# Three edits to a planned order on one Trainium2 core: the last group's choice behind a block's gated product, the first rows a step later, x loads behind block rows

## Chip, cores and metric

The kernel runs on one core of one Trainium2 chip (trn2). The metric is the device time of one execution in microseconds, the median of several runs; lower is better. Engines are named as the profile names them: PE (TensorE matmuls) and PEld (its weight loads), DVE (VectorE), ACT (ScalarE), POOL (GpSimd), SP (SyncE, which here issues most of the DMAs).

## Reference

Two feed-forward half-steps with a causal attention between them, for x of shape 2 x 2048 x 256 in float32. Cut to what matters:

```python
def half_step(x):                    # x already layer-normed by the caller
    xln = ln(x, ln1_w, ln1_b)
    att_out = sigmoid(xln @ Wr) * (xln @ Wv) @ Wo
    state = xln @ Ws
    x = x + att_out
    h = ln(x, ln2_w, ln2_b)
    conf = sigmoid(h @ [conf_rwkv; conf_trans])           # three experts
    bids = conf * capital_shares * sigmoid(h @ w_diff) + h @ W_aff
    winner = argmax(bids)
    scale = conf[winner] / (conf[winner] + 1e-6)
    out_rwkv[e] = square(relu(h @ K_rwkv[e])) @ V_rwkv[e]  # e = 0, 1; 256 -> 1024 -> 256
    out_trans = (h @ W1 * sigmoid(state @ W2)) @ W3
    return x + all_out[winner] * scale
x = x + 0.5 * half_step(layernorm(x))
x = x + attention(layernorm(x))      # one head of 128, softmax over the causal past
x = x + 0.5 * half_step(layernorm(x))
```

Only the winner's output of a token counts, so the kernel computes each token's winner alone.

## The kernel before

All arithmetic is float32. The 4096 tokens are two segments of 2048 (one for each batch entry), and a segment is four groups of 512 tokens (four tiles of 128 rows). A half-step has two parts, which overlap.

The front (`front`, class `Group`) takes the eight groups, 0 to 3 of the first segment and 4 to 7 of the second, in turn: moments and norms (`start`, `norm1`, `norm2`), transposes (`columns`, L348), the products for sigmoid gate and value (`r` and `v`, L362 on PE, L427 on ACT, L433 on DVE: the gate product `gate_t`), `mix` (L443), and `route` (L469). Then `logits` (L496 to L509) and `choose` (L517 to L531: bids, winners, and running counts `upto`; its last winner instruction, L526, is kept as `lately["chosen"]`). `rank` (L537, L538) and `slot` turn counts into a place for each token, and `move` (L568) scatters the group's rows into `by_slot` in DRAM, sorted by expert. After the last group of a segment `finish` writes `steer`, the list of which block starts at which slot; SP reads its entries into registers (L932, L964).

The experts part (`experts`, class `Block`) works on blocks of 256 rows of one expert. Kinds are "gt" (the gated expert), "rw" (an rwkv expert) and "half" (128 rows). `load_rows` (L933) reads a block's rows from `by_slot` into one of three `rows_in` buffers; `load_weights` (L944, L946) reads an rwkv expert's `w_k` and `w_e`. `ready` prepares the rows (L976 on DVE, L977 on ACT), `columns` transposes them (L847 on PE, copied out by L354 on ACT), `first` does the first product (for a gt block two sets of matmuls at L863, the sigmoid L990 on ACT, and the gated product L995 on DVE; for an rwkv block L863, relu L1004, L1005), and `second` the second (L878) with `res` (L903) and the scatter to the result (L911 on POOL). The first segment's blocks are two gt and four rw, and the second's follow.

Each part is a Python generator, and the code around it interleaves them: while the front does the second segment's groups (4 to 7), the experts part begins on the first segment's blocks. The order on the engines comes from the order in which the generators record, rearranged by the framework's scheduler, so the number of bare `yield` steps decides what stands beside what. `PACE` is 3 (front steps for one experts step) and `PAUSE` is 6. `tc.issue_after(ins)` (in `behind`) puts an instruction behind another of the same engine, in order only, with no semaphore. Engines run their queues in order.

In `pipelined`, which runs the blocks, block n + 1's weights and block n + 2's rows are asked for when block n starts. Its head loads the rows of blocks 0 and 1, waits some steps, and calls `ready` and `columns` for block 0, bound behind the choice that was recorded last. Block 1's `ready` is also bound so; from block 2 on it is not.

PSUM has two pools: `p_mm` with six buffers for products and `p_tp` with two, which transposes (`ps_t`, `ps_bt`, `ps_route`), routing sums (`ps_rc`), ranks and counts share.

Near the end of the first half-step `ahead` fetches the four x groups of the first segment (`fetch`, L152, from `x_mid` where the blocks' results went) for the attention, and normalizes them (L281 and on) between the late blocks.

Of the kernel before, what the change touches and what calls it, by code (L numbers as in the profile page):

```python
# [78 lines left out]
def kernel(ctx: ExitStack, tc: tile.TileContext, a: dict, out: bass.AP):  # L79
# [13 lines left out]
    def token_tiles(t, g):  # L93
        return t[g * TG : (g + 1) * TG, :].rearrange("(t p) d -> p t d", p=P)
# [48 lines left out]
        eng.dma_start(t, ap.rearrange("(k p) n -> p k n", p=P))  # L143
        return t

    def fetch(work, seg, n, src, bufs, after=(), beside=None):

        rows = work.tile([P, TB, RW], F32, name="rows", bufs=bufs)
        seg["rows"].append(rows)
        seg["x"].append(rows[:, :, XR : XR + C])  # L150
        seg["in_rows"].append(rows)
        ins = nc.sync.dma_start(seg["x"][n], src).ins  # L152
        if beside is not None:
            tc.declare_no_dep(ins, group=beside, reason="what may still come there has it fetched again")
            tc.add_to_no_dep_group(beside, ins)
        wait_for(ins, after)
# [217 lines left out]
    class Group:  # L374
# [133 lines left out]
            else:  # L508
                nc.scalar.activation(self.conf, self.by_kind[:, 0 : E + 1, :], AF.Sigmoid)  # L509

        def choose(self):
            upto = self.seg["upto"]
            if self.n == 0 and self.seg["prior"] is not None:
                nc.vector.tensor_copy(upto[:, :, 0], self.seg["prior"]["upto"][:, :, ST])
            conf = self.conf[:, 0:E, :]
            bids = sort_pool.tile([P, E, TB], F32, name="bids")
            nc.vector.tensor_mul(bids, conf, shares)  # L517
            nc.vector.tensor_mul(bids, bids, self.conf[:, E : E + 1, :].to_broadcast([P, E, TB]))
            nc.vector.tensor_add(bids, bids, self.by_kind[:, E + 1 :, :])

            most = sort_pool.tile([P, 2, TB], F32, name="most")
            nc.vector.tensor_max(most, bids[:, 0:2, :], bids[:, 1:3, :])
            wins = self.wins = sort_pool.tile([P, E, TB], F32, name="wins")
            nc.vector.tensor_tensor(wins[:, 0, :], bids[:, 0, :], most[:, 1, :], ALU.is_ge)
            nc.vector.tensor_tensor(wins[:, 2, :], bids[:, 2, :], most[:, 0, :], ALU.is_gt)
            lately["chosen"] = nc.vector.scalar_tensor_tensor(  # L526
                wins[:, 1, :], wins[:, 0, :], 1.0, wins[:, 2, :], ALU.is_lt, ALU.subtract
            ).ins
            for t in range(TB):
                at = self.n * TB + t  # L530
                nc.vector.tensor_add(upto[:, :, at + 1], upto[:, :, at], wins[:, :, t])  # L531
# [216 lines left out]
    def front(work, segs, by_exp=-1, on_move=lambda: None, fill=()):  # L748


        todo = [
            Group(work, seg, n, (b * GB + n <= by_exp, b * GB + n < by_exp)) for b, seg in enumerate(segs) for n in range(GB)
        ]

        def at(i):
            return todo[i] if 0 <= i < len(todo) else None

        def move(group):
            group.move()
            on_move()  # L760

        todo[0].start()
        run(todo[0].norm1(TB // 2))
        yield
        todo[1].start()
        todo[0].columns()
        yield
        for m in range(KC):
            todo[0].r(m)
            yield  # L770
            todo[0].v(m)
            yield
        run(todo[1].norm1(0))
        for i, this in enumerate(todo):
            late, following, further = at(i - 1), at(i + 1), at(i + 2)
            if late and late.n == GB - 1:
                late = None
            this.route(0)
            if late:
                late.rank()  # L780
                yield
            this.mix()
            yield
            this.route(1)
            if following:
                following.columns()
                yield
            this.deviation()
            yield
            if following:  # L790
                following.r(0)
                yield

            if further:
                further.start()
                yield
            if late:
                late.slot()
                with tc.issue_after((further or this).guess):
                    move(late)  # L800
                yield
            this.norm2(late.made if late else None)
            this.logits()
            yield
            if following:
                following.v(0)
                yield
            this.choose()
            yield
            if following:  # L810
                following.r(1)
                yield
                following.v(1)
                yield
            if this.n == GB - 1:

                yield from fill
                if not following:
                    for _ in range(PAUSE):
                        yield  # L820
                this.rank()
                this.slot()
                yield
                move(this)
                yield from finish(this.seg)
            if further:
                yield from further.norm1(0, following.made)
                yield

    def experts(work, segs, dest, redo=None):  # L830
# [98 lines left out]
        def load_rows(b, at, n, c):  # L929

            rows = work.tile([P, NI, RW], F32, name="rows_in", bufs=3)[:, 0:n, :]
            slot = nc.sync.value_load(segs[b]["steer"][0:1, at : at + 1], min_val=0, max_val=SLOTS - BLK)  # L932
            ins = nc.sync.dma_start(rows[:, :, c:], slot_rows(slot, n, c)).ins  # L933
            if b == 0:
                moves = segs[1]["moves"]
                tc.declare_no_dep(ins, group=moves, reason="rows of the other segment's tokens")
                tc.add_to_no_dep_group(moves, ins)
            for seg in segs[: b + 1]:
                wait_for(ins, seg["moved"])
            return rows  # L940
# [8 lines left out]
        class Block:  # L949
# [36 lines left out]
            def first(self, following=None, early=False):  # L986

                if self.kind == "gt":
                    sig = work.tile([P, 2, BLK], F32, name="gt_sig", bufs=1)
                    nc.scalar.activation(sig, several(w_s2, 0, self.cols_y), AF.Sigmoid)  # L990
                    yield
                    if following:
                        following.ready(lately["chosen"] if early else None)
                    self.mid = work.tile([P, KC, BLK], F32, name="gated", bufs=2)
                    self.made = nc.vector.tensor_mul(self.mid, several(later["w_1"], 0, self.cols), sig).ins  # L995
                    yield
                    return
                n = self.cols.shape[2]
                self.mid = work.tile([P, HC, BLK], F32, name="hid", bufs=2)[:, :, 0:n]
                step = 2 * BLK // n  # L1000
                for j in range(0, HC, step):
                    ps = several(self.w[0], j, self.cols)
                    relu = work.tile([P, 2 * BLK], F32, name="relu", bufs=2).rearrange("p (j n) -> p j n", n=n)
                    nc.scalar.activation(relu, ps, AF.Relu)  # L1004
                    self.made = nc.vector.tensor_mul(self.mid[:, j : j + step, :], ps, relu).ins  # L1005
                    yield
                    if following and j == HC // 2 - step:
                        following.ready(self.made)
# [7 lines left out]
        def pipelined(todo):  # L1016

            todo[0].load_rows()
            todo[0].load_weights()
            yield  # L1020
            todo[1].load_rows()

            yield
            yield

            todo[0].ready(lately["chosen"])
            todo[0].columns()
            yield
            for i, block in enumerate(todo):
                if i + 1 < len(todo):  # L1030
                    todo[i + 1].load_weights()
                if i + 2 < len(todo):
                    todo[i + 2].load_rows()
                yield from block.first(todo[i + 1] if i + 1 < len(todo) else None, i == 0)
                if i + 1 < len(todo):
                    todo[i + 1].columns()
                    yield
                yield from block.second()
# [212 lines left out]
    with pool("experts0", "right") as expert_pool:  # L1251
# [63 lines left out]

        def ahead():
            for n in range(GB):
                fetch(front_pool, t0, n, token_tiles(x_mid, n), GB, s0["results"], s1["moves_out"])
                yield
            yield from normed()  # L1320

# [70 lines left out]
```

## Time and profile before

| | us |
|---|---|
| Median of 3 runs | 881.61 |
| The runs | 881.1, 881.61, 886.78 |
| The profiled execution, its own time | 888.6 |
| Its span, first to last instruction | 886.4 |
| PE busy, DVE busy, ACT busy, POOL busy in the span | 845.2, 467.0, 319.5, 184.8 |
| Mean granted PE clock | 0.987 |

Times in the profile are those of one profiled execution, in us from the start of its span. In a timeline line the first number is the start, the second the duration, then engine, source line, operation, the tile written and read, shapes, and how many instructions of the kind are merged; in brackets stands the idle time of that engine just before, and what ended it. A few stages to find one's way: the front of the first half-step runs alone until about 98, the experts part overlaps groups 4 to 7 until about 149, blocks alone run until 334, attention until about 625, and the second half-step repeats the pattern (groups 4 to 7 with blocks from about 640 to 692, blocks alone until 878).

### The profile page before, as it was taken

To read this page: it belongs to the slowest core of one execution; us is meant where nothing else is said; L and a number is where in the kernel's file an instruction comes from. 1 tells how busy PE (TensorE), PEld (TensorE's weight loads), DVE (VectorE), ACT (ScalarE), POOL (GpSimd) and SP (SyncE) were. 2 spreads that over 40 slices of the span, in tenths; PEclk is the share of its full clock that TensorE was granted. 3 is DMA by queue.
4 is the path that set the end of the run, shared out by engine and by line. 5 is a ranking of instruction groups with operands and counts; after the bars stand their busy time and mean duration, and the time that the engine had idled before them with its cause. 6 is when DMAs were issued, how large, how long until landed. Compare 5 with 4: busy or idle time off the path is not lost. (4 is left out here: it accounts for less than half of the span.)

```text
span 886.4 us, 12466 instructions
## 1 busy us (share of the span) xinstructions
PE 845.2 (95%) x4136; PEld 616.9 (70%) x4136; DVE 467.0 (53%) x1857; ACT 319.5 (36%) x694; POOL 184.8 (21%) x232
## 2 busy tenths in 40 slices
PE   6999999999999998999899999999999999999996
PEld 4556567888878895655565556556556788888885
DVE  3588867233235445577434676665866532233322
ACT  3333542333244332454333343433352233243321
POOL 3145244111131211001000102022223410221101
PEclk9999999999999998999999999999999999999998
DMA  9424637656188543000000001021374763539652
GB/s 296 168 96 180 250 128 269 235 174 230 49 317 288 168 141 102 1 0 1 0 1 1 1 0 72 24 96 72 122 261 176 254 224 133 181 103 329 202 166 71
DMA packets 66370, 123.71 MB, mean 140 GB/s; under 512 B 4718, under 2 KB 44526, under 8 KB 66288
## 3 DMA queue, kind: packets, MB, share of 16 engines
q1 hardware_dynamic: 55856, 87.46, 29.5%
q0 software_dynamic: 8384, 33.70, 9.6%
q10 hardware_dynamic: 2048, 1.58, 0.6%
q8 instruction: 37, 0.61, 0.3%
q14 instruction: 45, 0.37, 0.1%
HBM read 82.47 MB, written 38.68 MB: 137 GB/s over the span
## 5 line engine op out<-in xcount | busy, mean ns | idle before, releaser
L863 PE MATMUL ps_b<-cols,w_k 128*128 128x256 f32 (+1 forms) x768 | 157.4, 363 | 0.0
L878 PE MATMUL acc<-w_e,hid 128*128 128x256 f32 x704 | 156.5, 379 | 0.0
L863 PEld LDWEIGHTS ps_b<-cols,w_k 128*128 128x128 f32 x768 | 137.4, 191 | 17.2
L878 PEld LDWEIGHTS acc<-w_e,hid 128*128 128x128 f32 x704 | 131.5, 190 | 17.3 <-DVE hid L1005 0.6
L291 POOL TENSOR_TENSOR r<-ve,mhalf 128x4 f32<-128x4 f32 (+1 forms) x40 | 50.9, 1272 | 380.9 <-DVE ve L332 291.0
L1004 ACT ACTIVATE relu<-ps_b 128x512 f32<-128x512 f32 x88 | 52.0, 591 | 171.4 <-PE ps_b L863 171.3
L1005 DVE TENSOR_TENSOR hid<-ps_b,relu 128x512 f32<-128x512 f32 x88 | 60.7, 690 | 80.3 <-ACT relu L1004 78.0
L903 DVE SCALAR_TENSOR_TENSOR res<-acc,rows_in 128x256 f32<-128x256 f32 x68 | 30.1, 479 | 119.8 <-PE acc L878 119.8
L1195 PE MATMUL ps_o<-p_tr,v 128*128 128x512 f32 (+3 forms) x160 | 73.4, 544 | 6.1 <-DVE p_tr L1189 2.9
L568 POOL DMA_INDIRECT by_slot<-rows,slots x64 | 62.5, 977 | 32.5 <-issue 27.0
L362 PE MATMUL ps_p<-y_t,w_r 128*128 128x512 f32 x128 | 64.8, 625 | 1.0 <-ACT y_t L417 0.9
L911 POOL DMA_INDIRECT out_dram<-res,where x34 | 33.5, 986 | 152.4 <-DVE res L903 139.3
L1141 PE MATMUL ps_s<-k_t,q_t 128*128 128x512 f32 (+3 forms) x160 | 64.2, 529 | 0.0
L443 PE MATMUL acc<-w_o,gate_t 128*128 128x256 f32 x256 | 61.2, 390 | 2.0 <-DVE gate_t L433 2.0
L362 PE MATMUL ps_p<-y_t,w_v 128*128 128x512 f32 x128 | 62.3, 607 | 0.0
L911 POOL DMA_INDIRECT x_mid<-res,where x34 | 33.7, 993 | 128.5 <-DVE res L903 123.4
L1158 ACT ACTIVATE prob<-ps_s,shift 128x512 f32<-128x512 f32 (+3 forms) x72 | 43.6, 615 | 43.5 <-DVE shift L1154 43.5
L1150 DVE TENSOR_REDUCE top<-ps_s 128x1 f32<-128x512 f32 (+2 forms) x80 | 48.4, 606 | 15.4 <-PE ps_s L1141 14.5
L443 PEld LDWEIGHTS acc<-w_o,gate_t 128*128 128x128 f32 x256 | 48.2, 194 | 9.7 <-DVE gate_t L433 2.4
L354 ACT ACTIVATE cols<-ps_bt,lnp 128x256 f32<-128x256 f32 (+1 forms) x96 | 47.1, 552 | 12.8 <-PE ps_bt L847 12.6
L1141 PEld LDWEIGHTS ps_s<-k_t,q_t 128*128 128x128 f32 x160 | 29.1, 190 | 28.8 <-issue 25.8
L281 DVE BATCH_NORM_STATS2 stats<-rows 128x6 f32<-128x256 f32 x128 | 46.2, 411 | 5.4 <-DMA rows<-in_x_dram 5.4
(227 smaller groups left out, 1127.8 us busy)
## 6 DMA issues: line engine op xcount, KB each, us to landing
w_k<-in_K_rwkv_dram SPq DMA_DIRECT2D x24, 1024.0 KB, 6.5
w_e<-in_V_rwkv_dram SPq DMA_DIRECT2D x24, 1024.0 KB, 7.4
rows_in<-by_slot SPq DMA_DIRECT2D x20, 516.0 KB, 5.6
rows_in<-by_slot SPq DMA_DIRECT2D x12, 772.0 KB, 5.4
rows<-in_x_dram SPq DMA_DIRECT2D x8, 512.0 KB, 5.4
by_slot<-rows_in SPq DMA_DIRECT2D x3, 772.0 KB, 11.3
x_mid<-rows_in SPq DMA_DIRECT2D x1, 2048.0 KB, 15.9
rows<-x_mid SPq DMA_DIRECT2D x4, 512.0 KB, 6.8
```

The costliest lines, as they stand in the source:

```text
L291: guess = nc.gpsimd.tensor_tensor(r0[:, 0:n, :], ve[:, 0:n, :], mhalf[:, 0:n, :], ALU.pow)
L362: nc.tensor.matmul(ps, lhsT=w[:, k, m * P : (m + 1) * P], rhs=src_t[:, k, :], start=k == 0, stop=k == KC - 1)
L443: nc.tensor.matmul(acc[:, i, :], lhsT=self.gate_t[:, k, t * P : (t + 1) * P], rhs=w_o[:, k, :], start=k == 0, stop=k == KC - 1,)
L568: nc.gpsimd.indirect_dma_start(out=by_slot, out_offset=bass.IndirectOffsetOnAxis(ap=self.slots[:, t : t + 1], axis=0), in_=self.rows[:, t, :],
L863: nc.tensor.matmul(ps[:, j, :], lhsT=w[:, k, (m0 + j) * P : (m0 + j + 1) * P], rhs=cols[:, k, :], start=k == 0, stop=k == KC - 1,)
L878: nc.tensor.matmul(acc[:, i, :], lhsT=src[:, j, i * P : (i + 1) * P], rhs=w[:, j, :], start=j == 0, stop=j == n - 1,)
L911: ins = nc.gpsimd.indirect_dma_start(out=dest, out_offset=bass.IndirectOffsetOnAxis(ap=where[:, i : i + 1], axis=0), in_=res[:, i, :], in_ ...
L1004: nc.scalar.activation(relu, ps, AF.Relu)
L1005: self.made = nc.vector.tensor_mul(self.mid[:, j : j + step, :], ps, relu).ins
L1141: nc.tensor.matmul(ps[:, :w], lhsT=seq["q_t"][:, qi * P : (qi + 1) * P], rhs=seq["k_t"][:, c * TG : c * TG + w], start=True, stop=True,)
L1150: nc.vector.reduce_max(top[:, c : c + 1], ps[:, :w], axis=AX.X)
L1195: nc.tensor.matmul(ps_o[:, i0 * P :], lhsT=seq["v"][:, j, :], rhs=p_tr[:, i0 * P :], start=j == 0, stop=j == blocks - 1,)
```

## The change

Three places. In `front` the choice of the very last group of a half-step (the one with no group after it) is recorded six steps later and its first instruction is put behind the newest gated product of a gt block on DVE; the pause between choice and rank is cut from six steps to three. In `pipelined` the first block's `ready` and `columns` come after three steps where they came after two, so that the choice to which `ready` is bound can be that of the next group. In `ahead` each fetch of x is put behind the newest load of block rows in SP's queue. `lately["load"]` and `lately["gated"]` are new entries for that. No instruction is added to or taken from the work on tiles.

```diff
--- before.py
+++ after.py
@@ -143,13 +143,14 @@
         eng.dma_start(t, ap.rearrange("(k p) n -> p k n", p=P))
         return t
 
-    def fetch(work, seg, n, src, bufs, after=(), beside=None):
+    def fetch(work, seg, n, src, bufs, after=(), beside=None, behind_load=None):
 
         rows = work.tile([P, TB, RW], F32, name="rows", bufs=bufs)
         seg["rows"].append(rows)
         seg["x"].append(rows[:, :, XR : XR + C])
         seg["in_rows"].append(rows)
-        ins = nc.sync.dma_start(seg["x"][n], src).ins
+        with behind(behind_load):
+            ins = nc.sync.dma_start(seg["x"][n], src).ins
         if beside is not None:
             tc.declare_no_dep(ins, group=beside, reason="what may still come there has it fetched again")
             tc.add_to_no_dep_group(beside, ins)
@@ -508,13 +509,14 @@
             else:
                 nc.scalar.activation(self.conf, self.by_kind[:, 0 : E + 1, :], AF.Sigmoid)
 
-        def choose(self):
+        def choose(self, after=None):
             upto = self.seg["upto"]
             if self.n == 0 and self.seg["prior"] is not None:
                 nc.vector.tensor_copy(upto[:, :, 0], self.seg["prior"]["upto"][:, :, ST])
             conf = self.conf[:, 0:E, :]
             bids = sort_pool.tile([P, E, TB], F32, name="bids")
-            nc.vector.tensor_mul(bids, conf, shares)
+            with behind(after):
+                nc.vector.tensor_mul(bids, conf, shares)
             nc.vector.tensor_mul(bids, bids, self.conf[:, E : E + 1, :].to_broadcast([P, E, TB]))
             nc.vector.tensor_add(bids, bids, self.by_kind[:, E + 1 :, :])
 
@@ -805,7 +807,13 @@
             if following:
                 following.v(0)
                 yield
-            this.choose()
+            if following or "gated" not in lately:
+                this.choose()
+            else:
+
+                for _ in range(PAUSE):
+                    yield
+                this.choose(lately["gated"])
             yield
             if following:
                 following.r(1)
@@ -816,7 +824,7 @@
 
                 yield from fill
                 if not following:
-                    for _ in range(PAUSE):
+                    for _ in range(PACE):
                         yield
                 this.rank()
                 this.slot()
@@ -930,7 +938,7 @@
 
             rows = work.tile([P, NI, RW], F32, name="rows_in", bufs=3)[:, 0:n, :]
             slot = nc.sync.value_load(segs[b]["steer"][0:1, at : at + 1], min_val=0, max_val=SLOTS - BLK)
-            ins = nc.sync.dma_start(rows[:, :, c:], slot_rows(slot, n, c)).ins
+            ins = lately["load"] = nc.sync.dma_start(rows[:, :, c:], slot_rows(slot, n, c)).ins
             if b == 0:
                 moves = segs[1]["moves"]
                 tc.declare_no_dep(ins, group=moves, reason="rows of the other segment's tokens")
@@ -993,6 +1001,7 @@
                         following.ready(lately["chosen"] if early else None)
                     self.mid = work.tile([P, KC, BLK], F32, name="gated", bufs=2)
                     self.made = nc.vector.tensor_mul(self.mid, several(later["w_1"], 0, self.cols), sig).ins
+                    lately["gated"] = self.made
                     yield
                     return
                 n = self.cols.shape[2]
@@ -1020,8 +1029,8 @@
             yield
             todo[1].load_rows()
 
-            yield
-            yield
+            for _ in range(3):
+                yield
 
             todo[0].ready(lately["chosen"])
             todo[0].columns()
@@ -1315,7 +1324,7 @@
 
         def ahead():
             for n in range(GB):
-                fetch(front_pool, t0, n, token_tiles(x_mid, n), GB, s0["results"], s1["moves_out"])
+                fetch(front_pool, t0, n, token_tiles(x_mid, n), GB, s0["results"], s1["moves_out"], lately["load"])
                 yield
             yield from normed()
```

## The prediction

> **What bounds the kernel now.** I read the page first (engine shares, the clock row), then the PE idle times over 0.25 us in the timeline, then the stretches around the largest. TensorE is the bound nearly everywhere:
>
> ```profile
> span 886.4 us, 12466 instructions
> ...
> PE 845.2 (95%) x4136; PEld 616.9 (70%) x4136; DVE 467.0 (53%) x1857; ACT 319.5 (36%) x694; POOL 184.8 (21%) x232
> ...
> PEclk9999999999999998999999999999999999999998
> ```
>
> No matmul is added or removed, so only PE's 41.2 us of idle time (886.4 - 845.2) and its half-clock stretches can move. Of these the first 8.1 us, the tail of 8.4 us and the gap of 4.10 us where attention begins (334.3) lie outside the change. Four stalls lie inside it. The first two are twins, one in each half-step; the timeline shows VectorE and PE there:
>
> ```profile
> 145.82 0.16 DVE L524 TENSOR_TENSOR wins<-bids,most 128x4 f32<-128x4 f32 x1
> 145.90 0.15 DVE L525 TENSOR_TENSOR wins<-bids,most 128x4 f32<-128x4 f32 x1
> 145.97 0.68 DVE L995 TENSOR_TENSOR gated<-ps_b,gt_sig 128x512 f32<-128x512 f32 x1
> 146.58 0.15 DVE L526 SCALAR_TENSOR_TENSOR wins<-wins 128x4 f32<-128x4 f32 x1
> ...
> 146.71 0.70 PE L878 MATMUL acc<-w,gated 128*128 128x256 f32 x2 [1.49 <-DVE gated L995]
> ...
> 690.86 0.70 PE L878 MATMUL acc<-w,gated 128*128 128x256 f32 x2 [1.50 <-DVE gated L995]
> ```
>
> The gated product stands in VectorE's queue behind most of the last group's choice, and PE waits for it. Where no choice is in the way, the same step (four transposes, then these matmuls) waits 0.41 us:
>
> ```profile
> 211.18 1.99 PE L878 MATMUL acc<-w,gated 128*128 128x256 f32 x8 [0.41 <-DVE gated L995]
> ```
>
> The third is in the second half-step only: VectorE waits for the first block's rows to land, a gate product queues behind them, and PE stops:
>
> ```profile
> 644.00 0.76 DVE L976 SCALAR_TENSOR_TENSOR rows_in<-rows_in 128x256 f32<-128x256 f32 x2 [2.47 <-DMA rows_in<-by_slot]
> 644.68 0.74 DVE L433 SCALAR_TENSOR_TENSOR gate_t<-ps_p,b_rv,sig 128x512 f32<-128x512 f32 x1
> ...
> 645.48 4.68 PE L443 MATMUL acc<-w_o,gate_t 128*128 128x256 f32 x14 [2.00 <-DVE gate_t L433]
> ```
>
> The fourth is near the end of the first half-step, where SP issues three loads of x ahead of a block's rows:
>
> ```profile
> 248.36 1.47 SPq L152 DMA_DIRECT2D rows<-x_mid  x3
> ...
> 250.16 0.38 SPq L933 DMA_DIRECT2D rows_in<-by_slot  x1
> ...
> 258.25 0.76 DVE L976 SCALAR_TENSOR_TENSOR rows_in<-rows_in 128x256 f32<-128x256 f32 x2 [4.98 <-DMA rows_in<-by_slot]
> ...
> 259.36 0.33 PE L847 MATMUL ps_bt<-ident,rows_in 128*128 128x128 f32 x1 [1.19 <-ACT rows_in L977]
> ...
> 261.06 1.99 PE L878 MATMUL acc<-w,gated 128*128 128x256 f32 x8 [0.66 <-DVE gated L995]
> ```
>
> Two of the stalls are followed by a stretch at half clock. In these windows the columns are the length, the busy us of PE, PEld, DVE, ACT and POOL, the granted clock, and DMA:
>
> ```profile
> 143.16:146.57 3.41, 2.06 (x12) 1.59 (x10) 2.37 (x13) 1.78 (x4) 2.60 (x4) 1.00 0.70 246
> 146.58:149.98 3.40, 3.27 (x18) 2.98 (x19) 2.91 (x27) 0.00 (x0) 1.98 (x3) 1.00 0.83 328
> 641.51:644.91 3.40, 1.97 (x23) 1.12 (x22) 0.93 (x4) 0.45 (x1) 0.00 (x0) 1.00 0.99 384
> 644.92:648.33 3.41, 2.85 (x7) 2.32 (x8) 1.41 (x10) 2.69 (x6) 0.00 (x0) 0.50 0.98 294
> 689.30:692.70 3.40, 1.90 (x12) 1.73 (x12) 2.88 (x20) 1.02 (x2) 2.78 (x3) 1.00 0.78 314
> 692.71:696.11 3.40, 3.40 (x9) 2.69 (x8) 3.40 (x28) 0.00 (x0) 1.98 (x3) 0.50 0.62 237
> ```
>
> PE was busy 1.97 and 1.90 us in the windows before the half-clock ones, and 2.06 us in the one that got off free: the line lies close to these stalls.
>
> **The change, part by part.**
>
> *The choice behind the gated product (A).* In the changed order the gated product stands ahead of the bids. It needs its matmuls; those begin at 142.89, and elsewhere the product starts 2.0 us after them (243.68 to 245.68), so about 144.9, and PE resumes 0.42 us after the transposes instead of 1.49: 1.07 us, and 1.08 at 689. What waits instead is the choice. Behind it on VectorE are the running counts, on PE the rank matmuls, on POOL the last group's four scatters (L568), and on SP the reads of steer. The choice takes about 1.3 us after the product (144.96 to 146.73 is 1.77, less the 0.68 of the product, plus a cast of 0.16 that now stands in between). PE has three of the four matmuls ahead of the rank, 3 x 0.43 = 1.3 us, so the rank meets it nearly on time; I charge nothing, and without that cover 1.3 us. The scatters also move behind the block's two row writes (L911), about 4 us later; the rows of the second segment that need them are read from SP at 178.97, over 20 us after. SP's reads of steer now stand ahead of the third rwkv block's weights (issued 158.78 and 163.93 today, used from 177.8 and 184.9), its rows ahead of the reads: slack of over 12 us. Bounds of A: 0 if the product finds another wait (ScalarE's sigmoid), 1.5 us if all is gained, at each place.
>
> *Half clock.* After the stall at 689 PE was busy all of 3.40 us at 0.50: 1.70 us lost. After the one at 643, 2.85/2 = 1.43 us. If the gaps shrink to 0.42 and nothing, both go. The Trainium skill (TensorE: Matmul & The Clock Gate, section "What's actually happening") has the clock fall after an idle window of some 3.4 us; by that these shorter gaps would cost nothing beyond themselves and the sum below would be 3.1 us smaller. The trace disagrees, with 0.50 behind gaps of 2.00 and 1.50. That page of the Trainium skill also calls the window free-running, which agrees with equal gaps at 145 and 690 of which one alone was followed by half clock. My bounds here are 0 (the windows fall otherwise) and 4.8 (the twin at 145 pays 1.70 too in the runs of before).
>
> *First rows a step later (B).* The two L976 of the first block leave the place at 644.00 and go behind the choice of the next group. The gate product then starts when its matmuls end (641.8), before PE wants it: 2.00 us gone, and 1.43 of half clock. The price is in both half-steps. Four L976 (the first two blocks') now follow one choice, and a gate product (0.67 us apart) stands inside that choice. First half-step: the choice ended at 112.46, so 113.1; L976 0.42 and L977 0.55 make the rows ready at 114.1. PE, in the new order from 109.79: value and gate projection 2 x 1.72, four transposes 0.43, so it asks at 113.66 and waits 0.45. Then ScalarE has two column copies (1.0), two more L977 (1.05) and two copies (1.0) until 118.4, while the rank needs the PSUM buffer that they free at about 118.15: 0.25. Against that, PE's 0.16 wait for y_t at 125.94 goes, as matmuls move in there: 0.55 us lost. In the second half-step the same count gives 0.3 + 0.4 - 0.17, again 0.55. Bounds of this loss: nothing (order within these queues shifts) and 3.0 us a half-step, by the row where PE waits for ScalarE's rows at 89.7 (1.34 us of idle, then 3.41 us at half clock).
>
> *x loads behind rows (C).* The rows of the first late rwkv block now leave SP at about 249.4, when VectorE frees their buffer, and not behind 1.5 MB of x. With the 4.1 us that the rows before them took (243.23 to 247.35) they are there at 253.6, before VectorE asks (about 256). Gone are 1.19, 0.16 (a second transpose) and 0.66; the usual 0.42 stays: 1.59 us. The twin place in the second half-step, with no x loads, has 0.42 today. The x loads wait behind rows whose buffer comes free at 255.8 and 262: two leave near 257, two near 263; with 6.8 us to landing they are there by 270, and VectorE first reads them at 280.31. The weights behind them (w_k, w_e of the next block) are wanted at 275. I charge nothing; if that cover went, each us late would show at 280 on VectorE, not on PE, which wants x at 338. Bounds of C: 0 and 2.0.
>
> **Sum.** A -1.07 - 1.08, half clock -1.70 - 1.43, B -2.00 + 0.55 + 0.55, C -1.59: -7.77 us. The profiled execution took 888.6 us (span 886.4 and 2.2 around it) and would take 880.8. The median of the runs is 881.61, 7 us lower; I carry the difference over in full: 873.8 us.
>
> **Rivals.**
>
> *The clock does not follow (R1).* The stalls go, but the half-clock stretches were luck of the window, or another gap meets it: without 3.13 us the sum is -4.64, 877.0. For: the twin at 145 escaped. Against: both stretches sit right behind a stall that goes. The Trainium skill's rule above (TensorE: Matmul & The Clock Gate) would give this case too.
>
> *The late data was the profile's (R2).* The unprofiled runs are 7 us faster, and B's and C's stalls are waits for transfers. If rows land in time there, C is 0 and B only costs 1.1 us with A's 2.15 left: -1.05, 880.6. For: the 7 us. Against: rows behind 1.5 MB of x stay late at the 361 GB/s that the stretch from 250 to 260 shows.
>
> *The new queue stalls PE (R3), the slower side.* The four L976 behind one choice, with PE's transposes and the rank behind them and only two PSUM buffers between, may stall PE for far longer than 0.55. The largest such event in the trace is the gap at 334.3: 4.10 us idle and 6.10 us of work at half clock (3.05), 7.15 us. At both places that is +14.3 in place of +1.1: the sum is +5.4, 887.0. It decides from 4.4 us a place (7.77 + 1.1, halved). Against: choice and copies there are rows of 0.16 to 0.55 us, and I found waits under 0.5.
>
> **How the numbers follow.** The measurement can tell about 1% (8.8 us, so 872.8 and 890.4) from no change. Forecast: 0.52, its own range 870 to 877, somewhat under half of it (0.25) below 872.8. R1: 0.22, of which 0.02 falls below 872.8. R2: 0.15. R3: 0.11, of which 0.07 beyond 890.4 if both places fall into several half-clock windows. So faster 0.27, same 0.66, slower 0.07. The range takes the forecast, R1 and R2 in: 868.5 to 882.5; what it leaves out is R3 and a little below.
>
> **What would show it.** Right: L878 after the transposes at about 145 and 680 waits near 0.42 us; no L976 waits for a transfer ahead of a gate product near 640, and L443 there has no idle time; rows before x in SP's list near 250, the 1.19 gone; PEclk without 0.50 near 640 and 690. B's price: idle of 0.3 to 0.5 us before L847 transposes near 113 and 650. Wrong: a PE gap over 1.5 us at those transposes or at the rank; L281 on x waiting for a transfer at 280; weights of the third rwkv block landing after 177.

## Result and profile after

The changed kernel takes 876.01 us (median of 9 runs, 875.35 to 878.85); the runs of before beside it have a median of 886.62 (9 runs, 880.9 to 888.43). The ratio over the runs is 0.9908, 95% interval 0.9881 to 0.9936 (the two medians alone would give 0.988, since before's runs are spread from 881 to 888). A later session on another chip gave 876.02 against 882.27: 0.9917 (0.9888 to 0.9946). On a third chip the same kernel was slower than before, 1.0046 (1.0029 to 1.0063); that is told with the experiments and bounds everything said here.

The profiled execution took 875.35, its span is 873.2, 13.2 less than that of before. The page of the changed kernel:

```profile
span 873.2 us, 12470 instructions
...
PE 838.0 (96%) x4136; PEld 612.6 (70%) x4136; DVE 468.0 (54%) x1857; ACT 318.8 (37%) x694; POOL 185.3 (21%) x232
...
PEclk9999999999999999999999999999999999999999
```

PE's busy time fell by 7.2 us with the same 4136 matmuls: that is the clock. Behind A's place in the second half-step, six instructions of the product on w_k (128x256) take 2.52 us at a granted clock of 0.50 in before (from 693.98), and 13 take 3.05 us at 1.00 in the changed kernel (from 681.99). The rest, 6 us, is idle time. Lines moved by eight or so: L878 is now L886, L995 is L1003, L976 is L984, L847 is L855, L433 and L443 are L434 and L444. The timeline at the two places of part A:

```profile
143.07 0.69 DVE L1003 TENSOR_TENSOR gated<-ps_b,gt_sig 128x512 f32<-128x512 f32 x1
...
143.68 0.16 DVE L519 TENSOR_TENSOR bids<-sig,shares 128x12 f32<-128x12 f32 x1
...
143.82 1.56 PE L886 MATMUL acc<-w,gated 128*128 128x256 f32 x6 [0.41 <-DVE gated L1003]
...
679.57 1.13 PE L886 MATMUL acc<-w,gated 128*128 128x256 f32 x4 [0.41 <-DVE gated L1003]
```

The product stands ahead of the bids, and both waits are 0.41 us. At the place of part B in the second half-step the output matmuls have no bracket, so no idle time ahead of them:

```profile
635.54 0.75 DVE L434 SCALAR_TENSOR_TENSOR gate_t<-ps_p,b_rv,sig 128x512 f32<-128x512 f32 x1 [0.42 <-PE ps_p L363]
...
636.39 3.70 PE L444 MATMUL acc<-w_o,gate_t 128*128 128x256 f32 x16
```

At the place of part C the rows leave ahead of x in SP's list. Those of the block that waited before leave at 246.85, and VectorE starts on them 4.2 us later; behind three loads of x that took 8.1 us (250.16 to 258.25 of before). The transposes at 255.34 find them, and the usual 0.41 is left. The next block's rows follow at 253.15, and two loads of x behind them:

```profile
246.85 0.37 SPq L941 DMA_DIRECT2D rows_in<-by_slot  x1
...
251.05 0.42 DVE L984 SCALAR_TENSOR_TENSOR rows_in<-rows_in 128x256 f32<-128x256 f32 x1 [0.84 <-DMA rows_in<-by_slot]
...
253.15 0.37 SPq L941 DMA_DIRECT2D rows_in<-by_slot  x1
253.83 1.02 SPq L153 DMA_DIRECT2D rows<-x_mid  x2
...
255.34 0.60 PE L855 MATMUL ps_bt<-ident,rows_in 128*128 128x128 f32 x4
...
256.35 1.99 PE L886 MATMUL acc<-w,gated 128*128 128x256 f32 x8 [0.41 <-DVE gated L1003]
```

And the clock behind the old places (columns as before: length, busy us of PE, PEld, DVE, ACT, POOL, clock, DMA):

```profile
640.20:643.63 3.43, 3.26 (x28) 1.85 (x21) 3.18 (x18) 1.36 (x3) 1.01 (x1) 1.00 1.07 405
...
681.20:684.60 3.40, 3.40 (x19) 3.07 (x19) 3.33 (x25) 0.60 (x1) 2.49 (x4) 1.00 0.93 313
```

How much of the 13.2 us the change owns is seen by laying the start of each PE instruction over the same one of before. From 24 us on, where no instruction differs, it is already 2.2 us ahead: the first, slow stretch ended earlier. The profile's record of the clock begins only at 23.7 us in before and at 19.0 in the changed kernel, and the same four instructions take 3.46 us ahead of that point and 1.96 behind it:

```profile
20.66 3.46 PE L362 MATMUL ps_p<-y_t,w_v 128*128 128x512 f32 x4
...
19.95 1.96 PE L363 MATMUL ps_p<-y_t,w_v 128*128 128x512 f32 x4
```

Another 1.75 us come where attention begins (one half-clock stretch of 3.41 us in place of two), and 0.5 in the tail; 0.4 is given back near 91, where the half-clock stretch falls on other instructions. So some 4 us are luck of the clock, and about 9 us lie at the changed places.

### The profile page after: what moved, and what is told of

The parts are those of the page before. It is cut to its first block, busy times and chain, and to the rows that moved or that the text cites. A ratio compares the mean times of both kernels' runs of the same rounds, so it can differ in the third digit from the quotient of the medians.

```text
span 873.2 us, 12470 instructions
## 1 busy us (share of the span) xinstructions
PE 838.0 (96%) x4136; PEld 612.6 (70%) x4136; DVE 468.0 (54%) x1857; ACT 318.8 (37%) x694; POOL 185.3 (21%) x232
## 5 line engine op out<-in xcount | busy, mean ns | idle before, releaser
L886 PE MATMUL acc<-w_e,hid 128*128 128x256 f32 x704 | 156.9, 380 | 0.0
L886 PEld LDWEIGHTS acc<-w_e,hid 128*128 128x128 f32 x704 | 131.4, 190 | 17.2 <-DVE hid L1014 0.6
L444 PE MATMUL acc<-w_o,gate_t 128*128 128x256 f32 x256 | 59.5, 384 | 0.0
L444 PEld LDWEIGHTS acc<-w_o,gate_t 128*128 128x128 f32 x256 | 47.4, 190 | 6.9 <-issue 0.8
L355 ACT ACTIVATE cols<-ps_bt,lnp 128x256 f32<-128x256 f32 (+1 forms) x96 | 47.2, 552 | 13.2 <-PE ps_bt L855 12.7
```

Source lines behind the costliest of these rows:

```text
L444: nc.tensor.matmul(acc[:, i, :], lhsT=self.gate_t[:, k, t * P : (t + 1) * P], rhs=w_o[:, k, :], start=k == 0, stop=k == KC - 1,)
L886: nc.tensor.matmul(acc[:, i, :], lhsT=src[:, j, i * P : (i + 1) * P], rhs=w[:, j, :], start=j == 0, stop=j == n - 1,)
```

## Experiments

Two sums are used below, from every timed run. A run's clock loss is its span times (1 - its mean granted clock); the rest, span times clock, is its time at full clock. Both are rough: the slow stretch ahead of the first record (19 to 26 us in the traces) counts as full clock, and the loss takes in a half-clock stretch behind the last matmul, 1.3 to 3.0 us by trace, that costs nothing. Runs of one kernel scatter by 1 to 1.9 us in the second sum. A difference from before has a standard error of 0.4 to 0.8 us in it and of 0.4 to 1.0 in the clock loss. Before has 874.5 at full clock and 7.0 us of clock loss (35 runs on one chip), and 874.4 and 7.1 (19 runs on another).

**Each part alone, and a filled gap** (one chip, before 883.33).

```
e1: the edits in choose, front and first (A)
e2:  -yield -yield  +for _ in range(3): yield      (B)
e3: the edits in fetch, load_rows and ahead (C)
```

> Only part A: the last group's choice is bound behind the block's gated product; rows and x loads stand as before. Theory (stalls and the half clock behind them): the product starts about 2.0 us after its matmuls, so the two waits of the gated matmuls behind the transposes (1.49 and 1.50 us before) shrink to about 0.42, -2.15 us together, and no 0.50 clock follows them; the row wait of 2.00 us near 643 and the 1.19 near 259 stay, and half clock may still follow the 2.00. Time -2.1 to -3.9 us, about 0.3%. Rival R1 (clock does not follow): idle -2.15, a 0.50 window still somewhere near 690, time -2.1. Rival (only the place of the wait changes): PE waits about 1.1 us at the rank matmuls that follow, time unchanged.

Measured: 881.08 us, ratio 0.9974 (0.9953 to 0.9995). At full clock -2.0 us, clock loss -0.4. The two waits are 0.42; the 2.00 near 643 stays (1.86, near 639) and is followed by a 0.50 stretch. A's idle came as priced; nothing moved to the rank behind it. A wait of 0.59 us at the rank matmuls of an earlier group, near 99, stands in this trace alone.

> Only part B: the first block's two row products stand a step later, behind the next group's choice. Theory as predicted: the wait of 2.00 us ahead of the output matmuls near 643 goes (and the half-clock stretch of 1.43 behind it), 0.55 us of new idle in each half-step at the first blocks' transposes and the rank: -0.9 us to -2.3. Theory after the changed kernel's trace: the choice ends before its block's transposes want rows, so the new idle is 0.1 us, not 0.55: -2.0 of idle, -3.4 with the half clock. Rival R2 (late rows are the profile's own): the profile shows -2.0 and the timed runs no gain or +0.2. Rival R3: over 4 us of PE idle near 113 or 650, slower. The waits of 1.49 and 1.50 and the 1.19 near 259 stay.

Measured: 885.33 us, ratio 1.0016 (0.9997 to 1.0035). At full clock -0.3, clock loss +1.6. The 2.00 near 643 is gone, and three waits are new or longer. The timeline of this run:

```profile
114.30 0.33 PE L847 MATMUL ps_bt<-ident,rows_in 128*128 128x128 f32 x1 [1.74 <-ACT rows_in L977]
...
686.61 0.16 DVE L526 SCALAR_TENSOR_TENSOR wins<-wins 128x4 f32<-128x4 f32 x1
686.69 0.68 DVE L995 TENSOR_TENSOR gated<-ps_b,gt_sig 128x512 f32<-128x512 f32 x1
686.92 0.36 PE L537 MATMUL ps_rank<-wins,before 128*128 128x12 f32 x2 [1.88 <-DVE wins L526]
```

With the rows a step later, the last group's choice stands wholly ahead of the gated product, and the rank matmuls ahead of the gated ones: PE waits 1.89 and 1.88 us there, not 1.49 and 1.50. So B alone makes A's stall worse, by 0.40 and 0.38, and a half-clock stretch followed the second. The 1.74 at 112 is taken up below.

> Only part C: the next half-step's x loads are bound behind the latest block's rows in SP's queue. Theory: the waits of 1.19, 0.16 and 0.66 us near 259 become one of about 0.41, -1.6 us, and nothing comes back before 338, since x is first read near 280 and lands by 270. A 2.0 us drift is possible if matmuls that stalled loads had slowed go too. The 1.49, 2.00 and 1.50 stay, each with or without a 0.50 window behind it. Rival R2: unchanged time beside a smaller profile. Rival (the loads are missed later): an idle of PE or VectorE at the norm of the next half-step near 280, or at the third rwkv block's weights.

Measured: 882.71 us, ratio 0.9979 (0.9955 to 1.0003). At full clock -2.4, clock loss +1.0. The three waits near 259 became one of 0.42, and PE has no new wait up to attention. In the changed kernel VectorE reads the fetched x at 275.60 and waits for nothing there.

```
e4:  before, with four matmuls between the transposes and the gated matmuls
  ps = p_mm.tile([P, C], F32, name="ps_fill", tag="mm")
  ... nc.tensor.matmul(ps, lhsT=ident, rhs=w_s2[:, 0, :], start=True, stop=True)
```

> The kernel before, with four matmuls (128x128 by 128x256, identity by a weight) added between the transposes and the gated matmuls, in both half-steps; nothing reads their product. They take 4 x 0.43 = 1.72 us in which PE waited 1.49 and 1.50 before, so no time is gained at the place itself: +0.1 to +0.4 us each, since the rank matmuls now stand ahead of the gated ones. What differs is only that PE is busy. Theory (half clock follows the idle): PE busy +3.0 us, idle -2.6, and the stretch of 3.41 us at 0.50 near 692 does not come, so the time falls by 0 to 1.5 us though work was added; the one near 645 stays. Rival R1 (half clock is luck of the window, not of these waits): 0.50 near 692 or at some other place as often as before, time +0.2 to +0.8.

Measured: 884.12 us, ratio 1.0007 (0.9987 to 1.0026). The timeline shows PE busy through the old gap (a matmul is two instructions here):

```profile
686.48 0.60 PE L855 MATMUL ps_bt<-ident,rows_in 128*128 128x128 f32 x4
686.91 1.89 PE L163 MATMUL ps_fill<-w_s,ident 128*128 128x256 f32 x8
688.74 0.36 PE L545 MATMUL ps_rank<-wins,before 128*128 128x12 f32 x2
```

No half-clock stretch came near 692, and none behind the wait of 1.92 us near 642, but one came near 261, behind a wait of 2.01 us at C's place. Over 12 runs the clock loss fell by 0.8 us (standard error 0.6), while the time at full clock rose by 1.4. That fits a busy PE that spares some half clock, but doesn't show it; and it puts what the two stalls carry together at about 0.8 us, not at the 1.70 that one of them carried in the profiled execution. The hoped-for fall in time did not come.

**The parts in pairs, and the change again** (another chip). Here before itself takes 897.03 us, 14 more.

```
e5: A and B    e6: A and C    e7: B and C    e8: the changed kernel
```

> Parts A and B without C. The parts alone moved the median by -2.25 (A), +2.0 (B) and -0.6 us (C), together some -1, while the whole change moved it by far more. Theory (A repairs what B breaks): with B alone the rank matmuls wait 1.89 and 1.88 us for the last group's choice near 145 and 685; with A in it too these places wait 0.42, and B's 2.00 near 643 is gone, so the idle falls by 1.07 + 1.08 + 2.00 = 4.15 us and the half-clock stretches behind 643 and 690 with it: about 877 to 879 in the session of the parts, C's 1.6 us above the whole change. Rival (the parts simply add, and the first comparison was lucky): about 883. Second point: B's first rows at 112 wait 1.3 to 1.8 us for late rows where no 0.50 stretch stands near 91, and about 0.1 where one does.

> Parts A and C without B. Theory (A repairs what B breaks): no repair is needed here, so the parts add: -2.15 and -1.6 of idle, the 2.00 near 643 stays with its half clock in some executions: 879.5 to 881.5, 3 to 4 us above the whole change. Rival (the interaction lies between A and C): within 1 us of the whole change.

> Parts B and C without A. Theory (A repairs what B breaks): the two waits of about 1.9 us at the rank matmuls stay, each with a 0.50 stretch behind it in some executions; about 883 to 884, 6 to 8 us above the whole change although A alone was worth 2. Rival (the interaction lies between B and C): within 3 us of the whole change.

> The changed kernel as it is, once more, beside its parts on one chip. Theory (A repairs what B breaks): 875.5 to 878 against a before of 883 to 884, so -6 to -8 us where the parts alone add up to -1. Rival (the parts add, and the first comparison was lucky with its half-clock stretches): 881 to 882. In the trace: if no 0.50 stretch stands near 91 this time, the first blocks' transposes near 112 wait 1.3 to 1.8 us for late rows and the end comes no sooner for it; if one does, 0.1 as in the first trace.

Measured: A and B 905.62, ratio 1.0101 (1.0074 to 1.0128); A and C 898.24, 1.0005 (0.9989 to 1.0022); B and C 898.78, 1.0029 (1.0013 to 1.0044); the change 900.98, 1.0046 (1.0029 to 1.0063). Every time expected was missed, by 14 us and more. What the traces settle: in both kernels with A the places of the gated product wait 0.42 us whether B is in or not, and in B and C without A the rank waits 1.89 twice. That A repairs what B breaks is thus shown as a stall; the times could not show it, because other stalls stand in all four traces. The timeline of the changed kernel there:

```profile
150.08 0.18 DVE L680 SCALAR_TENSOR_TENSOR steer<-second,valid 128x18 int32<-128x18 f32 x1 [0.48 <-DVE one L696]
151.48 0.16 DVE L689 TENSOR_TENSOR has<-left,more 128x2 f32<-128x2 f32 x1 [1.21 <-DVE steer L680]
...
157.20 0.60 ACT L1013 ACTIVATE relu<-ps_b 128x512 f32<-128x512 f32 x1 [12.21 <-remote]
...
161.84 0.47 PE L855 MATMUL ps_bt<-ident,rows_in 128*128 128x128 f32 x1 [7.91 <-ACT rows_in L985]
...
640.44 0.27 ACT L480 COPY by_col<-ps_rc 128x128 f32<-128x128 f32 x1 [3.88 <-remote]
640.76 1.11 PE L349 MATMUL ps_t<-ident,rows 128*128 128x128 f32 x4 [2.56 <-ACT by_col L480]
```

The second line is VectorE waiting 1.21 us for a 0.18 us instruction of its own ("remote" is a wait whose releaser the profile doesn't name); in the first trace of the changed kernel the two stand 0.09 us apart. ScalarE starts on a product at 157.20 that it started on at 148.25 there. For some 8 us signals come late, and PE waits 7.91 us for rows whose product stands behind VectorE's bookkeeping. It happens again near 704 (7.87). VectorE waits over 0.3 us for itself 2 to 12 times in each of these four traces, and never in a trace of the first comparison, of the parts alone or of the three kernels that follow. The stall is 7.9 and 7.9 us with A and B, 5.6 and 5.6 with A and C, 3.4 and 2.4 with B and C. In all four, half-clock stretches follow. The last two lines are a third place: near 638 PE waits 2.6 to 2.9 us in all four traces for a copy of 0.27 us that ScalarE starts late, again with a half-clock stretch behind it. No trace without late signals has that wait.

**The change a third time, before's trace, and a norm moved ahead** (a third later chip, before 882.27).

> The changed kernel once more. On the chip of its first trace it stood 0.92% under before; on the chip of the last four runs it stood 0.46% over it, with idle of 7.9 us at two transposes (near 154 and 704) where every signal between engines was late. Theory (the late signals are that chip's): a trace without such idle comes with 875 to 879 against a before of 881 to 887, ratio 0.990 to 0.994; a trace with it comes with a ratio over 1.000. Rival (they are the changed kernel's, in some executions on every chip): the idle near 154 in a trace whose before stands near 883.

Measured: 876.02, ratio 0.9917 (0.9888 to 0.9946); no late signals. At full clock -5.4 us against before, clock loss -1.4. The late signals belong to chips, then, or to the sessions on them (each chip was met in one), not to chance executions of the kernel.

> The kernel before, for its trace on this chip. If signals are late here as on the chip of the last four runs, before pays too, near 156 and 709, but less than the changed kernel's 7.9 us: the 14 us by which its median stood higher there, over two places and the half clock behind them, make 3 to 5 us of idle each. If they are not late here, the stalls of the first trace (1.49, 2.00, 1.50, 1.19) are found again within 0.2 us, and half-clock stretches behind some of them.

Measured: 881.29 in one run, a span of 879.1. Its stalls are 1.50, 0.75 and 0.66, 1.97 and 1.50: the first trace's, with 0.4 less at C's place. But no half clock follows the 1.97 or the 1.50s. So this pair of spans, the change at 877.4 and before at 879.1, shows the idle time at the changed places without their half clock. The changed kernel starts 2.6 us behind, since its first, slow stretch ended later (24.8 us and not 19.6). By the starts of the same PE instructions it gains nothing at B's first place (2.40 us behind to 2.36), 1.1 at A's first, of which 0.2 is given back by 157, 1.6 at C's, 2.2 at B's second, and 1.0 net at A's second: 5.7 us, if the 1.3 us that it loses from the start of attention to 640 (two half-clock stretches in place of one) is left out.

```
e11: in the changed kernel, at a segment's end
+  if further: yield from further.norm1(0, following.made); yield
   yield from finish(this.seg)
-  if further:
+  elif further: (the same, for the other groups)
```

> The changed kernel, with the next group's first norm recorded ahead of the scatter and bookkeeping of the segment that ends there. It aims at the wait near 87.5 us that all traces share (0.65 and a few of 0.16 us, rows of ScalarE that come late behind that bookkeeping on VectorE, and a 0.50 stretch behind it in most traces). If that is the cause: idle -0.8 to -1.3 there, no 0.50 near 91, and with the half clock -1 to -3 us. Rival (the order behind it shifts): the last group's choice falls ahead of the gated product or the rank again, 1.5 to 1.9 us near 144 and 680, and the gain is gone.

Measured: 882.43, ratio 0.9989 (0.9966 to 1.0012). The rival: the wait near 87 went, and 2.17 us (near 102) and 1.89 twice at the rank (144 and 682) came. The order that A and B make together is upset by one step; this is no better version.

**Three matmuls at the segment's border** (a fourth later chip, before 894.44).

```
e12: in the changed kernel, after route(1) of the second segment's first group
+  spare = p_mm.tile([P, C], F32, name="ps_fill", tag="mm")
+  for _ in range(3): nc.tensor.matmul(spare, lhsT=ident, rhs=w_o[:, 0, :], start=True, stop=True)
```

> The changed kernel with three matmuls (identity by a weight, 3 x 0.43 = 1.29 us) added near 87 us ahead of the transposes where PE waits 0.65 + 3 x 0.16 us for ScalarE's rows; nothing reads their product, and every other instruction keeps its place on its engine. Half clock theory: PE is busy where a 0.50 stretch followed in all traces of the changed kernel (near 91 to 93); the stretch goes, 1.3 us of PE time there. Then two theories of the wait of 1.74 us at the first blocks' transposes near 112, which part B alone showed and the changed kernel's traces did not, though both have the same order of instructions up to there. Landing theory: that wait is for rows that land at a time set by the loads, and PE only comes too early when it was spared the half clock; here it shows again, 1.2 to 1.8 us, and the time stays within 0.5 us of the changed kernel (876.0). Rival (the wait in part B alone was one execution's slow transfer): 0.1 us of wait near 112, and 874.3 to 875.

Measured: 899.5, ratio 1.0058 (1.0036 to 1.0081); late signals as on the slower chip above, with 7.7 us of idle near 153 and 703, so only the first 113 us can be read. The timeline:

```profile
87.46 1.56 PE L791 MATMUL ps_fill<-w_o,ident 128*128 128x256 f32 x6
...
93.75 2.05 SPq L946 DMA_DIRECT2D rows_in<-by_slot  x3
...
101.95 0.42 DVE L989 SCALAR_TENSOR_TENSOR rows_in<-rows_in 128x256 f32<-128x256 f32 x1 [1.74 <-issue]
...
112.08 0.33 PE L860 MATMUL ps_bt<-ident,rows_in 128*128 128x128 f32 x1 [1.35 <-ACT rows_in L990]
```

The half-clock stretch near 91 is gone, and the wait near 112 is there again, 1.35 us, as the landing theory has it. The third block's product on VectorE, which is bound to no choice, starts 8.2 us after SP issues the first of three row loads. In all traces but e11's it is 7.9 to 8.4 us, whatever PE's place: 93.74 to 101.89 in the changed kernel's first trace, 95.95 to 104.16 in part B alone. The profile gives "issue" for the wait of 1.74, so that it is the third load is inferred: in part B alone that load leaves at 97.63 and lands 6.4 us later, 0.2 us ahead of the product. Behind this product VectorE has the choice, and behind that the first rows, 9.0 to 9.2 us later in these three traces. So a PE that is spared the half clock comes early, and the first rows still wait until the loads land.

Open: the pairs were not run on a chip without late signals. No version beat the changed kernel.

## Why the prediction was right, and where it was not

The forecast of 873.8 us lies 2.2 us under the median of 876.0, inside its range, and the side is right where signals are not late. The terms, against the two sums:

| term | predicted | measured |
|---|---|---|
| idle and order, sum | -4.64 | -5.4 (full clock, third chip; standard error 0.7); -5.7 in the pair of traces there |
| A | -2.15 | -2.0 alone; -1.9 in the pair |
| B | -2.00 + 1.10 | -0.3 alone; -2.2 with A, in the pair |
| C | -1.59 | -2.4 alone (standard error 0.6); -1.6 in the pair |
| half clock | -3.13 | -1.4 (clock loss, third chip; standard error 0.9) |
| all | -7.77 | -6.8 (means of the runs, third chip); -8.1 in the first comparison |

- **A** failed in no step: 1.49 and 1.50 became 0.41, the rank met the choice on time. Its bound of 0 (ScalarE's sigmoid in the way) did not come true.
- **B, the 2.00 us**: right. **B, the price of 0.55 in each half-step**: mis-sized, it is about nothing. I had 0.45 of wait at the first transposes; the first trace has 0.13 at 112.05. In before's time, 1.8 us later, PE asks at 113.85 and not at 113.66, and the rows are ready at 113.98 and not at 114.1. The step that failed is the 0.25 for the rank's buffer: ScalarE's copies end at 115.98, matmuls on w_s stand ahead of the rank until 116.45, and it starts at 116.45 without a wait. The 0.16 at y_t went as put, so nothing is left; in the second half-step PE waits nowhere near the first blocks but the 0.17 that before has too. A price exists, 1.35 and 1.74 us, in the two traces with B where no half clock slows PE near 91, and there it takes back what the clock gave; in the five where one does, the wait is 0.12 to 0.14. (The bound of 3.0 us a half-step rests on a slip: the idle from 89.7 on adds up to 1.14 us, not 1.34.)
- **C** as predicted: the rows are read 4.2 us after they leave (4.1 was put), and no x load is missed. Its size moves with the run: the wait at the first transposes, 1.19 where it was priced, is 0.62 to 2.01 us in five other traces without C. By PE's starts C gained 2.0 us in the first pair of traces and 1.6 in the later one, 0.4 more in each than the waits in brackets add up to. Products that follow one another without a wait overlap in the timeline (251.88 + 1.89 and 253.61 in the changed kernel), and the sum of brackets leaves that out.
- **Half clock**: half clock behind such gaps, now and then, fits the traces, though it is argued from how often the two coincide; the size was too large by a factor of more than two. The step that failed is counting 1.70 and 1.43 in full from the one execution that was profiled, though the twin at 145 had escaped. In the nine traces without late signals there are 18 gaps of 1.49 to 2.17 us at such places, and 7 have a half-clock stretch behind them: none of five near 144, two of five near 640, three of five near 685. The two places of A and the one of B, at 7 in 18 of 1.70, 1.70 and 1.43 us, give an estimate of 1.9, and place by place 1.6; the runs give 1.1 to 1.4. Nor does the line hold that the prediction saw near 2 us of busy PE in a window: of windows laid like its own, those at 112.45 and 143.17 of part B alone had PE busy for 1.67 and 1.93 us and were followed by full clock, and the one at 685.87, with 2.21 us, by 0.50. The Trainium skill (TensorE: Matmul & The Clock Gate, "What's actually happening") asks for an idle window of some 3.4 us; here seven gaps of 1.50 to 2.17 us had half clock behind them, so the rule is too kind. The Trainium skill's free-running window agrees with equal gaps faring differently, and every half-clock stretch here lasts 3.41 us or a multiple, save the last of a run.
- **R1** (877.0) lies 1.0 us from the median, nearer than the forecast itself: less than half of the priced half clock went. **R2** fell: B's and C's stalls are in every trace without late signals that lacks those parts; C's removal shows in runs (-2.4), and B's in the pair of traces. **R3** fell as put: no stall of 4.4 us at the first blocks. The only slower outcome came from elsewhere.
- **What no rival had**: the slack of 12 us that I gave the reads of steer and the rows behind them. Where signals are late, the rows of the first block after the last group come 7.9 us late in the changed kernel, at both places. That A lengthens this by putting the choice, and with it the bookkeeping, later is what the lengths suggest (5.6 to 7.9 with A, 3.4 and 2.4 without); before's own trace on such a chip is missing, so it is argued, not shown.
- **The carried 7 us** between the profiled execution and the median: before's median itself moved between 882 and 887 with the sample, and its fastest and slowest runs differ by their clock (0.994 and 0.987 in many). The profiled execution had a clock loss of 11.5 us, and runs of before have 7.0 on average, so more than half of the 7 us carried was half clock, as was my -3.13; starting from runs that had little of it and taking it off again counted some of it twice. I read the missing 2.2 us so; no run separates them. That the forecast came so near owes something to luck: the idle time gave 0.8 us more than put (5.4 for 4.64), which covered part of the half clock that didn't go.

## To carry to other kernels

Price a half-clock stretch by how often such gaps have one, over several traces or by the mean granted clock of the runs, not by the one execution that was profiled. Edits in one order of queues don't add: a step that moves rows can push a choice in front of another wait, so test them in pairs, and against the part that was alone worth little. A wait hidden behind a slower engine is still there, and a gain ahead of it is taken back by it.

## Not expected of the hardware

- One kernel, two kinds of chip (or of session on it): before has medians of 882 to 887 in three sessions and 894 to 897 in two others. In the traces of those two, VectorE waits 0.3 to 1.5 us for its own instructions, and other engines start late, for some 8 us twice in a run; PE waits 2.5 to 2.9 us near 638 besides. In the changed kernel DMA moves 367 and 384 GB/s in those two stretches; in its first trace the first of them runs at 394 GB/s with no such wait, and in A and C's trace the late signals come at 211 and 224 GB/s, so the rate alone doesn't do it. What does stays open.
- A gap of 0.65 + 3 x 0.16 us near 87 to 90 was followed by a half-clock stretch in 6 of the 8 traces without late signals that have it in this form.
